# Attention scores of a graph layer: from sums of rows and columns to products of exponentials, spread through DRAM

## The chip, the cores and the metric

The kernel runs on one core of a Trainium2 chip. The metric is the time of one execution on the device in microseconds (us). Its engines are TensorE (PE; its weight loads are shown apart as PEld), VectorE (DVE), ScalarE (ACT), GpSimd (POOL) and SyncE (SP, which here only issues DMAs). Each runs its own instructions in order; semaphores tie them together.

## The reference

For 64 graphs of 256 nodes with 256 features: a graph-attention layer pair (GAT) with a feed-forward part, then a relational attention layer with a feed-forward part. The change touches only the GAT softmax, which runs twice per graph:

```python
def _gat(h, adj, W, a, out_features):
    Wh = jnp.matmul(h, W)
    Wh1 = jnp.matmul(Wh, a[:out_features])
    Wh2 = jnp.matmul(Wh, a[out_features:])
    e = Wh1 + jnp.swapaxes(Wh2, 1, 2)
    e = jax.nn.leaky_relu(e, negative_slope=ALPHA)      # ALPHA = 0.2
    scores = jnp.where(adj > 0, e, NEG)
    att = jax.nn.softmax(scores, axis=1)
    return jnp.matmul(att, Wh)
h = _gat(x, adj, W1, a1, Fout)
h = _gat(h, adj, W2, a2, W2.shape[1])
h = _layernorm(residual + h, g_ln1, b_ln1)
```

After it come a ReLU feed-forward (256 to 1024 to 256) with a layernorm, then 8-head attention whose weights are masked by the relation, a projection, a layernorm, a GELU feed-forward and a layernorm. All values are float32.

## The kernel before

**Tiles.** Two graphs make a group (G = 2, 512 nodes), so there are 32 groups. The nodes of a group lie on 128 partitions in T = 4 blocks, two blocks a graph (NB = 2). "Transposed" tiles such as `xT` and `hT` hold features on partitions.

**The pipeline.** `turn(y_, x_, z)` (L1226) is one turn of the main loop (L1533) and works on three groups at once: group `y_` is in its relational attention and GELU feed-forward, group `x_ = y_ + 1` in the ReLU feed-forward, group `z = y_ + 2` in its two GAT layers. So 30 of the 32 groups pass their GAT layers in a turn; groups 0 and 1 do it ahead of the loop (L1499 to L1510). In the turns where all three groups exist, the order of PE, SP, DVE and ACT is the order in which `turn` writes the instructions (L1271). Where a step is placed in `turn` is therefore where it stands in the queue of each engine.

**Group z in a turn.** `early` transposes the loaded x, `project` (L1145) multiplies it by the weights and two score vectors into `xp` (a 128x260 product and an ACT copy per block; the last columns hold the row and column scores). It is split: two blocks ahead of `first("4b")`, two blocks behind `out_(0)`. `first_scores` (L1149) makes a `Softmax` object for layer 1, and `score_rows` (L745) turns the row scores on PE: four transposes of a column that is repeated 128 times give a PSUM bank with the row of 512 scores on every partition. Then per graph `b`:

- `scores(b)` (L764): ACT adds the column score as a bias to the row for two blocks (L766), DVE applies the leaky function over 128x512 (L768).
- `exp(b)` (L770): ACT takes the exponential over 128x512.
- `masks(b)` (L773): DVE multiplies each block by the adjacency and sums the block's rows into `z` (L775).

`shares` (L778) inverts `z`, `scaled` (L789) multiplies xp by it on ACT, and `first_sums` (L1167) multiplies the scores with xp on PE (`hpp`, L800) into `hp`. Layer 2 does the same from `hp`: `second_scores` is called after the GELU part, its `scores` and `exp` stand between the products of the second feed-forward, and `second_sums` (`ygp`, L811) ends it.

**Neighbours in the queues.** Between those steps stand the other groups' steps. `sums(n)` are the attention sums of a head group on PE (`po`, `zo`), `shares(b)` their division on DVE (L1123 to L1128), `out_(b)` the output projection with its addition (L814). `first(...)` and `second(...)` are the seven products of a Strassen-like hidden layer (`hidden_seven`, L869): products 1, 6, 7, 4 accumulate in one PSUM bank and DVE adds that bank into `h` after 1, 6 and 7 (L910), before the next product goes into it; 2, 5, 3 use another bank, copied by ACT (L907). `out(n)` and `out.sums(n)` are the seven products of the output layer (L987), their additions (L995) and operand sums (L973). `normed_features` (L689) transposes 32x32 squares on DVE (L694) and places them with 12 DMAs and four POOL copies (L713, L711); layer `2` splits the DMAs between SP and ACT. `stored` and `load_rows` issue the 512 KB store of a finished group (L1202) and the 512 KB load of the next rows (L441) on SP. `affine` is two DVE passes over 128x1024 (L864, L867).

**Buffers.** SBUF tiles come from pools by tag; tag `es` has two buffers of 4 KB a partition and serves the sums over nodes and the division; tag `v` has one, shared by the values of the attention and the scores `s`. PSUM tag `g` has six banks, which all of the above share.

Of the kernel before, what the change touches and what calls it, by code (L numbers as in the profile page):

```python
# [9 lines left out]
F32 = mybir.dt.float32  # L10
I32 = mybir.dt.int32
AF = mybir.ActivationFunctionType
ALU = mybir.AluOpType
# [3 lines left out]
P = 128  # L17
NEG = -9000000000000000.0
ALPHA = 0.2
# [366 lines left out]
def narrow_path(  # L386
# [13 lines left out]
    nc = tc.nc  # L400
    B, N, F = x.shape
# [3 lines left out]
    KB = F // P  # L405
    FB = FF // P
    NB = N // P
    G = 2
    T = G * NB
    TN = G * N  # L410
# [68 lines left out]
    high = const.tile([P, T], F32, name="high")  # L479
    nc.gpsimd.memset(high, 0.0)  # L480
    other = const.tile([P, NG], F32, name="other")

    def weight(w, name):
        t = const.tile([P, w.shape[0] // P, w.shape[1]], F32, name=name)
# [172 lines left out]


    mark = {}

    def behind(*names):

# [82 lines left out]
    def score_rows(u, l, wh, c):  # L745

        rows = bank(f"rows{u}_{l}")
        for t in range(T):
            nc.tensor.transpose(rows[:, t * P:(t + 1) * P],
                                wh[:, t, c:c + 1].to_broadcast([P, P]), ident)  # L750
        return rows

    class Softmax:

        def __init__(s, u, l, wh, rows, c):
            s.u, s.wh, s.rows, s.c = u, wh, rows, c
# [4 lines left out]
        def block(s, b):  # L761
            return s.s[:, b * NB:(b + 1) * NB, :].rearrange("p t n -> p (t n)")

        def scores(s, b):  # L764
            for t in range(b * NB, (b + 1) * NB):
                nc.scalar.activation(s.s[:, t, :], s.rows[:, b * N:(b + 1) * N], AF.Identity,  # L766
                                     bias=s.wh[:, t, s.c:s.c + 1])
            nc.vector.scalar_tensor_tensor(s.block(b), s.block(b), ALPHA, s.block(b), op0=ALU.mult, op1=ALU.max)  # L768

        def exp(s, b):  # L770
            nc.scalar.activation(s.block(b), s.block(b), AF.Exp)

        def masks(s, b):  # L773
            for t in range(b * NB, (b + 1) * NB):
                nc.vector.scalar_tensor_tensor(s.s[:, t, :], s.s[:, t, :], 1.0, g[s.u]["aT"][:, t, :],  # L775
                                               op0=ALU.mult, op1=ALU.mult, accum_out=s.z[:, t:t + 1])
# [4 lines left out]

        def all(s):
            for b in range(G):
                s.scores(b)
                s.exp(b)
                s.masks(b)
            s.shares()

# [69 lines left out]
    def affine(y, g_, b_):  # L858

        times(y, g_)  # L860
        plus(y, b_)
# [144 lines left out]
    class Projections:  # L1006
# [111 lines left out]
    def divided(u, b, po, zo, oT):  # L1118


        rz = work.tile([P, KB * N], F32, tag="es", name=f"rz{u}_{b}")
        rq = work.tile([P, KB * N // 32], F32, tag="rq", name=f"rq{u}_{b}")
# [22 lines left out]
    def project(z, blocks=range(T)):  # L1145
        d = g[z]
        d["xp"] = projected(z, d["xT"], blocks, d.get("xp"))

    def first_scores(z):  # L1149
        d = g[z]  # L1150
        d["m"] = Softmax(z, 0, d["xp"], score_rows(z, 0, d["xp"], F + 2), F + 3)

    def second_scores(z):
        d = g[z]
        d["m"] = Softmax(z, 1, d["hp"], score_rows(z, 1, d["hp"], F), F + 1)

    def first_softmax(z):
        first_scores(z)
# [67 lines left out]
    def turn(y_, x_, z):  # L1226
# [46 lines left out]
        with order:  # L1273
# [73 lines left out]
            masks(3)  # L1347
            totals(3)
            if Z:
                project(z, range(0, T // 2))  # L1350
            first("4b")
            sums(2)
            sums(3)
# [5 lines left out]
                    out.sums(1, 2)  # L1359
            if Z:  # L1360
                shares(1)
            out_(0)
            if Z:
                mv = moments(y_, 2, y, range(NB))
# [1 line left out]
                n = norm(y_, 2, y, range(NB))  # L1366
            piece()
            if Z:
                project(z, range(T // 2, T))
            if Z:  # L1370
                early_adjacency(z)
            elif X:
                out.sums(1)
                out(1, 2)
                out.sums(2)
            out_(1)
            piece()
            if Z:
                first_scores(z)
            if Z:  # L1380
                n = norm(y_, 2, y, mv=mv)
            else:
                applied_norm(y, *n)
                n = norm(y_, 2, y, range(NB, T))
            if Z:
                out(1)
                Z["m"].scores(0)
                Z["m"].scores(1)
                Z["m"].exp(0)
                Z["m"].exp(1)  # L1390
                out.sums(4)
                out(2, 5)
            elif X:
                out(5)
                out.sums(3)
# [31 lines left out]
                n = moments(x_, 1, X["y"], range(NB))  # L1427
            if Z:
                first_sums(z, range(T // 2, T))
            if X:  # L1430
                out.product(4)
            tt = work.tile([P, HPB, NB * N], F32, tag="e", name=f"tt{y_}_1")
            second = hidden_seven(y_, 1, hT, w1s, b1, AF.Gelu, Y, tt.rearrange("p a n -> p (a n)"))
            if X:
                out.add(4)
                n = norm(x_, 1, X["y"], mv=n)
# [5 lines left out]
                applied_norm(X["y"], *n, [0])  # L1442
            if Z:
                affine(y, rg3, rb3)
            second("3a")
            if X:
                applied_norm(X["y"], *n, [1])
# [11 lines left out]
            if y_ >= NG - 2:  # L1459
# [129 lines left out]
```

## Time and profile before

| | |
|---|---|
| median of 3 runs | 3045.75 us (3045.45 to 3047.17) |
| profiled execution | 3043.91 us |
| its span | 3042.3 us |
| granted TensorE clock | 0.995 |
| ACT busy / POOL busy | 1684.9 us / 679.8 us |
| row transposes (L749), modelled busy | 39.9 us in 256 instructions |
| leaky function on DVE (L768) | 92.4 us in 128 |
| exponentials (L771) | 76.5 us in 128, and 30 table loads of 1283 ns |
| masks (L775) | 98.9 us with 128 accumulator reads |
| score biases on ACT (L766) | 100.3 us in 256 |

The profile is one execution recorded by the hardware. Its page gives each engine's busy time, the chain of work that ended last, the groups of instructions by line with their mean duration, and the DMA issues with their time to landing. A timeline shows one engine's instructions in order: start, length, engine, line, operation, tile written <- tiles read, shape, count, and in brackets how long the engine stood idle before it and what ended the idle time. PE's ends are modelled and overlap, so on PE the distance between two starts is the measure.

### The profile page before, as it was taken

Reading aid. Unit: us, or ns where it says so; the run is one execution under the profiler, and the core shown is the slowest. Engines: PE = TensorE matmul, PEld = TensorE weight load, DVE = VectorE, ACT = ScalarE, POOL = GpSimd, SP = SyncE. Lnnn points to the kernel's source line nnn. Section 1 sums busy time; section 2 is a strip of 40 time slices with the busy share of each in tenths; the row PEclk is TensorE's granted clock in tenths of the full one; section 3 lists DMA queues with packets and bytes.
Section 4 is the critical chain, followed back from the end, with each engine's and each line's share of the span. In section 5 each row is a group of like instructions: output and inputs, shape, how many; then the busy total and the mean of one; then the engine's idle time right before and its main releaser. Section 6 shows DMA issues by size and latency. Waiting matters only on the chain.

```text
span 3042.3 us, 58414 instructions
## 1 busy us (share of the span) xinstructions
PE 3000.0 (99%) x22192; PEld 2459.6 (81%) x22192; DVE 2645.7 (87%) x5025; ACT 1684.9 (55%) x3404; POOL 679.8 (22%) x930
## 2 busy tenths in 40 slices
PE   7999999999999999999999999999999999999998
PEld 6788888888787888787888878887878887878876
DVE  5788988888898889898889888898988898988887
ACT  4455555655655555555555455556555555555553
POOL 4222221222211222212222112222112222122211
PEclk8999999999999999999999999999999999999999
DMA  5011111211111211111111112111112111121000
GB/s 147 13 35 36 37 39 25 44 37 39 34 35 32 44 37 39 33 27 43 40 37 36 40 25 44 38 39 33 34 35 44 36 38 35 25 45 37 19 13 16
DMA packets 428402, 113.24 MB, mean 37 GB/s; under 512 B 364586, under 2 KB 427604, under 8 KB 428116
## 3 DMA queue, kind: packets, MB, share of 16 engines
q1 hardware_dynamic: 418076, 102.20, 15.3%
q10 hardware_dynamic: 8984, 6.19, 0.8%
q8 instruction: 178, 2.92, 0.4%
q0 software_dynamic: 1056, 1.05, 0.1%
q14 instruction: 108, 0.88, 0.1%
HBM read 56.78 MB, written 16.78 MB: 24 GB/s over the span
## 4 chain that ended last, share of the span: by engine, by line
PE 90%; DVE 7%; ACT 1%; DMA 1%; POOL 1%; issue 0%; SPq 0%; DVEq 0%; POOLq 0%; ACTq 0%
PE yf L987 22%; PE h1a L898 15%; PE h1b L898 12%; PE po L1112 8%; PE qk L1053 7%; PE v L1053 7%; PE sp L1084 4%; PE xpp L740 4%; PE yop L811 4%; PE ygp L811 3%; PE zo L1115 2%; PE hpp L800 2%; DVE s L775 2%; DVE yt L694 1%; DVE eaq L973 1%; DVE y L995 1%
## 5 line engine op out<-in xcount | busy, mean ns | idle before, releaser
L907 ACT COPY h<-h1b 128x512 f32<-128x512 f32 x384 | 224.5, 585 | 349.4 <-PE h1b L898 342.6
L910 DVE TENSOR_TENSOR h<-h1a,h 128x512 f32<-128x512 f32 x384 | 262.9, 685 | 114.6 <-PE h1a L898 108.8
L1097 DVE TENSOR_TENSOR ea<-e,aT 128x1024 f32<-128x1024 f32 x256 | 311.2, 1237 | 2.9 <-ACT e L1093 2.6
L855 ACT ACTIVATE y<-y,nm,rs 128x256 f32<-128x256 f32 x450 | 249.8, 597 | 114.4 <-DVE nm L845 110.1
L1093 ACT ACTIVATE e<-sp 128x512 f32<-128x512 f32 x512 | 270.8, 600 | 28.1 <-PE sp L1084 21.4
L1036 ACT COPY qk<-qk 128x512 f32<-128x512 f32 x128 | 75.1, 587 | 339.0 <-PE qk L1053 339.0
L711 POOL COPY hT<-yt 32x256 f32<-32x256 f32 x244 | 203.2, 833 | 184.9 <-DVE yt L694 172.6
L837 POOL TENSOR_SCALAR rs<-mv 128x4 f32<-128x4 f32 (+1 forms) x134 | 33.3, 248 | 841.0 <-DVE mv L827 625.3
L826 DVE BATCH_NORM_STATS2 st<-y 128x6 f32<-128x256 f32 x512 | 207.3, 407 | 4.5
L995 DVE TENSOR_TENSOR y<-yf,y 128x256 f32<-128x256 f32 x448 | 183.2, 409 | 29.5 <-PE yf L987 29.4
L1125 POOL TENSOR_TENSOR low<-low,rq 128x16 f32<-128x16 f32 x64 | 13.9, 218 | 810.4 <-DVE rq L1124 810.4
L867 DVE TENSOR_TENSOR y<-y,rb 128x1024 f32<-128x1024 f32 (+1 forms) x130 | 167.0, 1284 | 3.2
L941 ACT ACTIVATE h<-h,cols 128x512 f32<-128x512 f32 x256 | 167.0, 714 | 1.5 <-DVE h L910 1.1
L864 DVE TENSOR_TENSOR y<-y,rg 128x1024 f32<-128x1024 f32 (+1 forms) x130 | 161.6, 1243 | 1.2 <-ACT y L855 1.1
L1102 DVE TENSOR_TENSOR es<-e 128x1024 f32<-128x1024 f32 x128 | 155.8, 1217 | 0.0
L703 POOL COPY hT<-yt 32x256 f32<-32x256 f32 x120 | 114.9, 958 | 169.3 <-DVE yt L694 165.1
L838 POOL TENSOR_TENSOR rs<-rs,mhalf 128x4 f32<-128x4 f32 (+1 forms) x134 | 146.9, 1096 | 8.3
L1084 PE MATMUL sp<-qk 32*128 32x256 f32 x2048 | 146.6, 400 | 0.4 <-DVE qk L1040 0.3
L742 ACT COPY xp<-xpp 128x260 f32<-128x260 f32 x128 | 45.4, 385 | 172.6 <-PE xpp L740 172.5
L694 DVE STREAM_TRANSPOSE yt<-y 128x256 f32<-128x256 f32 x364 | 136.0, 418 | 4.5
L1112 PE MATMUL po<-e,v 128*32 128x256 f32 x2048 | 136.3, 384 | 0.0
L898 PE MATMUL h1a<-tt,wf 128*128 128x256 f32 x512 | 134.2, 386 | 0.3 <-DVE h L910 0.3
(280 smaller groups left out, 7589.6 us busy)
## 6 DMA issues: line engine op xcount, KB each, us to landing
hT<-yt SPq DMA_DIRECT2D x912, 32.0 KB, 1.9
y<-in_x_dram SPq DMA_DIRECT2D x32, 512.0 KB, 4.5
xq<-in_x_dram SPq DMA_DIRECT2D x240, 64.0 KB, 2.1
aq<-in_adj_dram SPq DMA_DIRECT2D x240, 64.0 KB, 2.3
out_dram<-y SPq DMA_DIRECT2D x30, 512.0 KB, 2.9
hT<-yt ACTq DMA_DIRECT2D x180, 32.0 KB, 1.9
wf<-in_L_gnn_w_ff_dram SPq DMA_DIRECT2D x2, 1024.0 KB, 7.6
w<-in_L_gnn_W_dram SPq DMA_DIRECT2D x2, 1024.0 KB, 7.9
```

The source lines that it names most:

```text
L811: nc.tensor.matmul(ps[:, i * F:(i + 1) * F], lhs(t, k), rhs(b, k), start=(k == 0), stop=(k == n - 1))
L855: mark["normed"] = nc.scalar.activation(y[:, t, :], y[:, t, :], AF.Identity, bias=nm[:, t:t + 1], scale=rs[:, t:t + 1])
L898: nc.tensor.matmul(ps[:, i * N:(i + 1) * N], w_[:, f * P:(f + 1) * P], m, start=first and i == 0, stop=True, skip_group_check=True)
L907: mark["copied"] = nc.scalar.copy(out(h, o, b), pair(ps))
L910: mark["added"] = nc.vector.tensor_tensor(out(h, o, b), pair(one[h]), out(h, o, b), ALU.add)
L987: nc.tensor.matmul(s.ps[n][:, i * F2:(i + 1) * F2], a[:, k, i * P:(i + 1) * P], w_[:, k, :], start=n in (1, 2, 5) and i == 0 and k == 0, s ...
L995: mark["out"] = nc.vector.tensor_tensor(yq, s.ps[n][:, :F].rearrange("p (i f) -> p i f", i=NB), yq, ALU.add)
L1053: nc.tensor.matmul(ps[:, i * N:(i + 1) * N], l, r, start=n in (1, 2, 5) and i == 0, stop=True, skip_group_check=True)
L1084: nc.tensor.matmul(ps[a][:, j * N:(j + 1) * N], k_[hp, m, j0:j0 + P], q[hp, m, b * N:(b + 1) * N], start=True, stop=True)
L1093: nc.scalar.activation(e[:, a, :], ps[a], AF.Exp, scale=isd)
L1097: nc.vector.tensor_tensor(ea[:, a:a + 2, :], e[:, a:a + 2, :], ab[:, None, :].to_broadcast([P, 2, NB * N]), ALU.mult)
L1112: nc.tensor.matmul(po[hp, m * N:(m + 1) * N], vs[:, hp], w[:, a, j * N:(j + 1) * N], start=(n == 0), stop=(n == len(terms) - 1))
```

## The change

The identity used is exp(leaky(r + c)) = max(exp(r) exp(c), exp(0.2 r) exp(0.2 c)), and a factor exp(c) that is common to a softmax row cancels: the weight becomes max(exp(r), exp(0.2 r) f) with f = exp(-0.8 c). So only the row and column scores are exponentiated, 128x4 numbers each, not the 256x256 sums.

- In groups 2 to 31, ACT takes three exponentials of 128x4 columns: `f`, and `k` with exp(r) and exp(0.2 r). `rows` (a new method) transposes `k` on DVE in 32x32 squares (each column repeated 32 times), writes the 1024 numbers to a line in DRAM by one DMA from four partitions, and reads that line onto all 128 partitions by a second DMA (512 KB, 4 KB a partition). Both are issued by SP.
- In groups 0 and 1 the rows are still turned by PE, and ACT exponentiates the PSUM bank twice.
- `masks(b)` makes each block by one DVE instruction (multiply by `f`, then the larger of that and the other row) before it multiplies by the adjacency as it did.
- The leaky function, the 128x512 exponentials and the Identity activations of `scores` are gone.
- `project(z)` is in one piece ahead of `first("4b")`, followed by `first_scores`; `rows` of layer 1 stands behind `shares(1)`; `out(1)` takes the place of the second half of the projection.
- `second_scores` stands right behind `first_sums`, its `rows` behind the operand sums of the second hidden layer, `masks(0)` of layer 2 between that layer's fifth and third products.
- A tiny exponential `warm` on ACT stands where the scores of layer 2 were exponentiated.
- The tile `rq` has one buffer in place of two.

```diff
+    dram = ctx.enter_context(tc.tile_pool(name="lines", bufs=2, space=bass.MemoryType.DRAM))
...
+        def __init__(s, u, l, wh, r):
...
+            nc.scalar.activation(s.f, wh[:, :, r + 1], AF.Exp, scale=ALPHA - 1.0)
+            if u > 1:
+                s.k = work.tile([P, 2, T], F32, tag="ek", name=f"ek{u}_{l}", bufs=1)
+                for n, scale in enumerate((1.0, ALPHA)):
+                    nc.scalar.activation(s.k[:, n], wh[:, :, r], AF.Exp, scale=scale)
+            else:
+                rows = score_rows(u, l, wh, r)
+                er = work.tile([P, 2, TN], F32, tag="es", name=f"er{u}_{l}")
+                for n, scale in enumerate((1.0, ALPHA)):
+                    nc.scalar.activation(er[:, n], rows, AF.Exp, scale=scale)
+                s.e = [er[:, n] for n in range(2)]
+
+        def rows(s):
+
+            tr = work.tile([P, 2 * T, 32], F32, tag="es", name=f"tr{s.n}")
+            nc.vector.transpose(tr, s.k.rearrange("p e t -> p (e t)")[:, :, None].to_broadcast([P, 2 * T, 32]))
+            er = work.tile([P, 2, T, Q, 32], F32, tag="es", name=f"er{s.n}")
+            line = dram.tile([2 * T, Q, 32], F32, tag="line", name=f"ln{s.n}")
+            nc.sync.dma_start(line.rearrange("n a y -> a n y"), tr[::32])
+            nc.sync.dma_start(er.rearrange("p e t a y -> p (e t a y)"),
+                              bass.AP(tensor=line.tensor, offset=line.offset, ap=[[0, P], [1, 2 * TN]]))
+            s.e = [er[:, n].rearrange("p t a y -> p (t a y)") for n in range(2)]
+
+        def masks(s, b):
+            bn = slice(b * N, (b + 1) * N)
             for t in range(b * NB, (b + 1) * NB):
-                nc.scalar.activation(s.s[:, t, :], s.rows[:, b * N:(b + 1) * N], AF.Identity,
-                                     bias=s.wh[:, t, s.c:s.c + 1])
-            nc.vector.scalar_tensor_tensor(s.block(b), s.block(b), ALPHA, s.block(b), op0=ALU.mult, op1=ALU.max)
-
-        def exp(s, b):
-            nc.scalar.activation(s.block(b), s.block(b), AF.Exp)
-
-        def masks(s, b):
+                nc.vector.scalar_tensor_tensor(
+                    s.s[:, t, :], s.e[1][:, bn], s.f[:, t:t + 1], s.e[0][:, bn], op0=ALU.mult, op1=ALU.max)
...
             if Z:
-                project(z, range(0, T // 2))
+                project(z)
+                first_scores(z)
             first("4b")
...
             if Z:
                 shares(1)
+                Z["m"].rows()
             out_(0)
...
             if Z:
-                project(z, range(T // 2, T))
-            if Z:
+                out(1)
                 early_adjacency(z)
...
-            if Z:
-                first_scores(z)
...
             if Z:
-                out(1)
-                Z["m"].scores(0)
-                Z["m"].scores(1)
-                Z["m"].exp(0)
-                Z["m"].exp(1)
                 out.sums(4)
                 out(2, 5)
...
                 first_sums(z, range(T // 2, T))
+                second_scores(z)
...
             second = hidden_seven(y_, 1, hT, w1s, b1, AF.Gelu, Y, tt.rearrange("p a n -> p (a n)"))
+            if Z:
+                Z["m"].rows()
...
                 affine(y, rg3, rb3)
+                Z["m"].masks(0)
             second("3a")
...
-            second_scores(z)
...
-            Z["m"].scores(0)
             out.add(1)
             out.product(5)
-            Z["m"].scores(1)
-            Z["m"].exp(0)
-            Z["m"].exp(1)
+            nc.scalar.activation(warm, mhalf[:, 0:1], AF.Exp)
             checked(z, Z["aq"])
...
-            Z["m"].masks(0)
             out(6)
             Z["m"].masks(1)
```

More of the change, by code (lines that the diff above doesn't have):

```diff
@@ L481, in narrow_path @@
     other = const.tile([P, NG], F32, name="other")
+    warm = const.tile([P, 1], F32, name="warm")
     def weight(w, name):
@@ L753, in narrow_path @@
     class Softmax:
-        def __init__(s, u, l, wh, rows, c):
-            s.u, s.wh, s.rows, s.c = u, wh, rows, c
+        def __init__(s, u, l, wh, r):
+            s.u, s.wh, s.n = u, wh, f"{u}_{l}"
             s.s = (work.tile([P, T, N], F32, tag="v", name=f"s{u}_{l}", bufs=1) if u > 1 else
@@ L759, in __init__ @@
             s.z = work.tile([P, T], F32, tag="z", name=f"z{u}_{l}")
-        def block(s, b):
-            return s.s[:, b * NB:(b + 1) * NB, :].rearrange("p t n -> p (t n)")
-        def scores(s, b):
-            for t in range(b * NB, (b + 1) * NB):
-                nc.scalar.activation(s.s[:, t, :], s.rows[:, b * N:(b + 1) * N], AF.Identity,
-                                     bias=s.wh[:, t, s.c:s.c + 1])
-            nc.vector.scalar_tensor_tensor(s.block(b), s.block(b), ALPHA, s.block(b), op0=ALU.mult, op1=ALU.max)
@@ L770, in exp @@
-        def exp(s, b):
-            nc.scalar.activation(s.block(b), s.block(b), AF.Exp)
-        def masks(s, b):
+            s.f = work.tile([P, T], F32, tag="ef", name=f"ef{u}_{l}", bufs=1)
+            nc.scalar.activation(s.f, wh[:, :, r + 1], AF.Exp, scale=ALPHA - 1.0)
[9 more added lines that the diff above has]
+                s.e = [er[:, n] for n in range(2)]
@@ L783, in all @@
             for b in range(G):
-                s.scores(b)
-                s.exp(b)
                 s.masks(b)
@@ L1121, in divided @@
         rz = work.tile([P, KB * N], F32, tag="es", name=f"rz{u}_{b}")
-        rq = work.tile([P, KB * N // 32], F32, tag="rq", name=f"rq{u}_{b}")
+        rq = work.tile([P, KB * N // 32], F32, tag="rq", name=f"rq{u}_{b}", bufs=1)
         nc.vector.transpose(rz, zo)
@@ L1150, in first_scores @@
         d = g[z]
-        d["m"] = Softmax(z, 0, d["xp"], score_rows(z, 0, d["xp"], F + 2), F + 3)
+        d["m"] = Softmax(z, 0, d["xp"], F + 2)
     def second_scores(z):
         d = g[z]
-        d["m"] = Softmax(z, 1, d["hp"], score_rows(z, 1, d["hp"], F), F + 1)
+        d["m"] = Softmax(z, 1, d["hp"], F)
     def first_softmax(z):
```

## The prediction

> **What bounds the kernel now.** I read the page first (busy shares, chain), then one settled turn of the loop as a timeline engine by engine, then the DMA issues.
>
> The page:
>
> ```profile
> span 3042.3 us, 58414 instructions
> ...
> PE 3000.0 (99%) x22192; PEld 2459.6 (81%) x22192; DVE 2645.7 (87%) x5025; ACT 1684.9 (55%) x3404; POOL 679.8 (22%) x930
> ...
> PE 90%; DVE 7%; ACT 1%; DMA 1%; POOL 1%; issue 0%; SPq 0%; DVEq 0%; POOLq 0%; ACTq 0%
> ```
>
> TensorE (PE) is never really idle, so a matmul removed is time saved, and anything that makes PE wait is time added. DVE at 87% is second. ACT at 55% has room.
>
> PE in the turn from 1033.34 to 1125.91 us (pitch 92.57 us; the turns around 812, 1459 and 2105 us show the same pattern):
>
> ```profile
> 1080.09 0.60 PE L749 MATMUL rows<-ident,xp 128*128 128x128 f32 x4
> 1080.52 3.74 PE L987 MATMUL yf<-wf,h 128*128 128x128 f32 x32
> 1084.10 3.74 PE L987 MATMUL yf<-wf2t,eq 128*128 128x128 f32 x32
> 1087.67 1.95 PE L987 MATMUL yf<-wf,eaq 128*128 128x128 f32 x16
> 1089.46 1.91 PE L800 MATMUL hpp<-xp,s 128*128 128x258 f32 x8
> ...
> 1103.86 1.89 PE L898 MATMUL h1a<-tt,w1s 128*128 128x256 f32 x8
> 1105.74 3.91 PE L898 MATMUL h1a<-tt,w 128*128 128x256 f32 x16
> 1109.48 0.60 PE L749 MATMUL rows<-ident,hp 128*128 128x128 f32 x4
> 1109.92 1.95 PE L987 MATMUL yf<-w,h 128*128 128x128 f32 x16
> ```
>
> Differences of starts are the real cost, since the ends overlap: the four row transposes cost 0.43 us and 0.44 us of PE, twice a turn. Two places have no slack. The aggregation `hpp` starts at 1089.46, when ACT has only just scaled xp (ACT L791 runs from 1088.59). Products 6a/6b need 1.88 us instead of 1.73 before 7a starts at 1105.74, because 7a waits for DVE's addition of 6a.
>
> DVE in the same turn:
>
> ```profile
> 1084.06 1.22 DVE L973 TENSOR_TENSOR eaq<-h,eq 128x1024 f32<-128x1024 f32 x1
> 1085.19 0.41 DVE L995 TENSOR_TENSOR y<-yf,y 128x256 f32<-128x256 f32 x1
> 1086.08 0.42 DVE L995 TENSOR_TENSOR y<-yf,y 128x256 f32<-128x256 f32 x1 [0.48 <-PE yf L987]
> 1086.42 0.15 DVE L845 SCALAR_TENSOR_TENSOR nm<-mv,rs 128x4 f32<-128x4 f32 x1
> ...
> 1102.53 1.47 DVE L867 TENSOR_TENSOR y<-y,rb 128x1024 f32<-128x1024 f32 x1
> 1104.99 0.69 DVE L910 TENSOR_TENSOR h<-h1a,h 128x512 f32<-128x512 f32 x1 [1.00 <-PE h1a L898]
> ```
>
> DVE has only 0.48 us of idle time ahead of the first layer's masks and 1.00 us ahead of the addition of 6a. These two gaps are all the cover that the new DVE work has.
>
> DMA issues (KB, us to landing), and SP around the second layer:
>
> ```profile
> hT<-yt SPq DMA_DIRECT2D x912, 32.0 KB, 1.9
> y<-in_x_dram SPq DMA_DIRECT2D x32, 512.0 KB, 4.5
> ...
> out_dram<-y SPq DMA_DIRECT2D x30, 512.0 KB, 2.9
> ```
>
> ```profile
> 1094.70 0.54 SPq L1202 DMA_DIRECT2D out_dram<-y  x1
> 1097.71 0.39 SPq L441 DMA_DIRECT2D y<-in_x_dram  x1
> ```
>
> The 512 KB load of the next rows goes out at 1097.71 (4.4 us to landing), just where the second layer's new DMAs will stand.
>
> **What the Trainium skill says.** "DMA: Bandwidth & Descriptors", section "Anatomy of one DMA", puts about 2.0 us fixed cost on a DMA, mostly the receipt of the write; the trace agrees (1.9 us for 32 KB). The same page, "Queues, rings and completion order": "On each SDMA engine descriptors are consumed in ring order", so a small DMA issued by SP behind a large one waits for it. The trace points the same way: at the start a 128 KB row load behind two 1 MB weights took 8.0 us, another 4.1. "ScalarE: Activation LUTs", "What ACT_TABLE_LOAD costs", has 1283 ns a load, the trace 1283 exactly, and 186 ns + 0.833 ns an element for an ACTIVATE without pointer operands: an estimate of 0.19 us for each new 128x4 exp, which the trace before does not show.
>
> **The change, part by part**, with the turn above as the clock.
>
> (1) Row transposes leave PE in 30 of 32 groups: 30 x (0.43 + 0.44) = 26 us saved if nothing else waits. The freed PSUM bank is worth nothing: I see no bank wait over 0.3 us here.
>
> (2) ACT loses four Identity (1.57 us) and two exps (1.2 us) a layer, gains three tiny exps (0.6 us by the estimate; 0 to 1). With 55% busy this is worth nothing directly. Table loads stay two a turn: `warm` takes the exp load (1.28 us) where L771 had it. They don't add.
>
> (3) DVE a layer: away two 128x512 leaky ops (1.28 us in layer 1), in come a 128x256 transpose (0.33 us pitch, as L694) and four 128x256 maxima. Their nearest row is L775, same engine, form and size: 0.345 us pitch, so 1.38 us. Net +0.43 us. More important is the place: the leaky ops ran early; the maxima sit directly in front of the masks.
>
> (4) First layer. The second half of the projection (1.75 us of PE) moves ahead of sums(2) and sums(3), so zo ends near 1076.5 instead of 1074.7 and DVE starts shares(1) at 1076.5, not 1075.34. From there its queue is solid, from its own rows: shares 2.38, transpose 0.35, out_(0) add and moments 1.78, add(1) 0.34, adjacency 1.14, out_(1) add and moments 1.85, sums(4) 1.13, two adds 0.68, which is 1086.15. The norm offset waits for GpSimd's pow (moments end + 2.0 us, as before) to 1086.4. Masks take 8 x 0.345 = 2.76, the reciprocal 0.15: 1089.4. ACT scales two blocks by 1090.4, and hpp's four first products end at 1091.75, 0.3 us later than before although PE was ready 0.43 earlier. DVE's transposes for hT end at 1091.15 instead of 1089.8, so all 12 hT DMAs, and SP behind them, slide by 1.35 us; the second hidden stage starts at 1097.45 instead of 1096.87. The broadcast itself is hidden: transpose out by 1079.3, line landed 1081.3 (1.9 us), spread landed 1085.7 (4.4 us), needed at 1086.5.
>
> (5) Second layer. SP's order is: hT, store, load of the rows, line, spread. The load now goes out at 1097.71 + 1.35 = 1099.05; DVE's transpose is done at 1099.25; so the line is issued right behind 512 KB. With ring order it lands when that load does, 1103.45. SP waits for it and then issues the spread. Its 512 KB in 4 KB pieces is not in the trace: lower bound the 512 KB store, 2.9 us; upper bound by the nearest row, 4.4 us with its 1 KB pieces; I take 4.0. Landed at 1107.5. DVE reaches masks(0) at 1105.1 (the affine 2.7 us behind the offset at 1102.4), so it waits 2.4 us; masks(0) 1.38, addition of 6a 0.69: 7a can start at 1109.6. PE was ready at 1106.3. Queued behind the waiting DVE: the additions of 6a, 6b, 7a, 7b, and behind those GELU and the output sums. Some turns (812, 2105) issue the load 0.7 us earlier; mean about 1109.25. Against 1105.74 that is +3.5; 0.43 comes back with the removed transposes: **+3.1 us a turn**. The rest of the turn has no new wait: the leaky ops and masks(0) have left DVE there, and the GELU chain shifts no more than PE does.
>
> (6) Prologue: groups 0 and 1 keep the PE transposes; ACT 2.8 us becomes two PSUM exps (1.2 us), DVE slightly more. I take -2 us (0 to -6).
>
> Sum: 28 turns x 3.1 = +87; the first and last such turns have no store or load in front of the line, and DVE alone costs about +1.2 each; prologue -2. Against the profiled execution (3043.91 us, of which the span is 3042.3): 3043.9 + 87 + 2.4 - 2 = 3131. The median of the runs is 1.8 us above that execution: **3133 us**.
>
> **The rivals.**
>
> A, the forecast (0.53): the line queues behind the row load. With the spread at 2.9 to 4.4 us and +-0.4 us on the queue sums, 2.0 to 3.9 us a turn: 3100 to 3155.
>
> B (0.25): the line is not held up by the load. It lands 1.9 us after issue (1101.4), the spread at 1105.4 to 1105.8, just when DVE arrives. Then only DVE's extra work counts: 7a at about 1107.2 to 1107.9, +1.0 to +1.7 a turn, 3074 to 3100; with a little more slack than I found, 3065. For it: the line needs few pieces and SP issues it just 0.4 us behind the load. Against: the ring order above.
>
> C, the other side, faster (0.10): PE is still the only bound, because DVE has more slack than my sums give it. Place: the addition of 6a. It decides from the point where the spread has landed and the affine is over by 1104.2, so that 7a starts at 1106.3, and where the first layer's masks are over by 1088. Then the 26 us are saved: 3045.75 - 26 - 2 = 3018. For it: 99% busy PE, 13% idle DVE. Against: both gaps on DVE are smaller than the work put in them.
>
> D (0.12): 128 reads of one 4 KB line are slower than an ordinary load. At 6.4 us (2 more) the first layer's masks are 1.2 us late too and the second layer's 3.6: about 6 us a turn, 3045.75 + 30 x 6 - 2 = 3224. Against: the 128 KB row broadcasts at the start ran within a stretch of 350 to 371 GB/s.
>
> Some 0.2% (6 us) is what a measurement of this kernel can tell from no change; between B and C I leave 0.03 for that, out of their 0.35. Chances: faster 0.09, same 0.03, slower 0.88.
>
> The range leaves out C and most of D: 3070 to 3180, which holds A, nearly all of B and the near end of D.
>
> **What would show it.** PE idle in front of hpp (about 0.7 us, on ACT xp) and in front of 7a (about 3 us, on DVE's addition into h); DVE idle in front of the second layer's first maximum, on the DMA er, about 2 us, and none in the first layer; line landing about 4 us in layer 2 and 2 us in layer 1; PE busy some 26 us less; maxima at about 0.41 us each. I am wrong if the line lands in 2 us in both layers (B), if PE shows no wait at 7a (C), or if DVE waits for er in the first layer as well (D).

## The result and the profile after

The changed kernel takes 3158.44 us (median of 4 runs, 3156.53 to 3164.04) against 3045.61 us (3045.45 to 3047.17) for the kernel before on the same chip: ratio 1.0373, interval 1.0356 to 1.0389. It is 112.8 us slower; the forecast was 3133 us with 3070 to 3180 as its range.

The head of the page of the kernel after: span, busy times, and the chain of work that ended last.

```profile
span 3154.9 us, 58139 instructions
...
PE 2987.0 (95%) x21952; PEld 2444.4 (77%) x21952; DVE 2688.9 (85%) x5213; ACT 1545.3 (49%) x3242; POOL 681.8 (22%) x930
...
PE 66%; DVE 19%; DMA 8%; POOL 2%; issue 2%; SPq 1%; ACT 1%; ACTq 0%; DVEq 0%; POOLq 0%
```

PE falls from 99% to 95% busy, and its part of the chain from 90% to 66%; DVE and DMA have taken over. PE has less work, and waits for more than it lost. What it waits for stands in the list of PE's waits of the kernel after (us in total, times, longest):

```profile
PE hpp L819 <- ACT xp L810: 51.0, 30, 1.8
PE h1a L917 <- DVE h L929: 50.4, 31, 3.5
PE yf L1006 <- DVE eaq L992: 20.4, 30, 0.7
```

Three waits a turn, 121.8 us in all. In the same list of the kernel before only the second has an entry, of 1.0 us in 3 times; that list begins with a 6.1 us wait of the prologue and goes on with sums of 4.9 us and less. The three are, in order of a turn: ahead of the aggregation (1.70 us, layer 1), ahead of output product 7 (0.68 us, layer 1) and ahead of hidden product 7a (1.63 us in the turn below, layer 2).

The turn that follows is the counterpart of the one in the prediction. I measure both from the start of the PE instruction `sp` just ahead of the turn's first projection (1066.43 us before, 1103.04 us after):

| PE instruction | before | after | slip |
|---|---|---|---|
| aggregation `hpp`, first half | 23.03 | 24.45 | 1.42 |
| output product 7 (`yf<-wf,eaq`, the second such) | 25.02 | 27.13 | 2.11 |
| second hidden stage, first product (`h1b<-hT,w`) | 30.44 | 32.55 | 2.11 |
| hidden product 7a | 39.31 | 43.06 | 3.75 |
| next turn's first `qk` | 59.48 | 62.84 | 3.36 |

So layer 1 costs 2.11 us and layer 2 another 1.64, of which 0.39 comes back. From the loop's first projection to its last, 29 pitches sum to 2681.9 us before and 2790.0 us after (+108.1, or 3.73 a turn); the first such projection starts 2.2 us later, and what lies behind the last is 2.3 us longer.

**Layer 1.** PE of the kernel after in that turn:

```profile
1123.84 1.95 PE L1006 MATMUL yf<-wf,eaq 128*128 128x128 f32 x16
1127.49 2.01 PE L819 MATMUL hpp<-xp,s 128*128 128x258 f32 x8 [1.70 <-ACT xp L810]
1130.17 2.05 PE L1006 MATMUL yf<-wf,eaq 128*128 128x128 f32 x16 [0.68 <-DVE eaq L992]
```

DVE in the same stretch tells why (`...` stands for rows left out):

```profile
1113.27 0.72 DVE L1142 STREAM_TRANSPOSE rz<-zo 128x512 f32<-128x512 f32 x1 [0.90 <-PE zo L1134]
...
1115.74 0.43 DVE L782 STREAM_TRANSPOSE tr<-ek 128x256 f32<-128x256 f32 x1
...
1121.11 1.19 DVE L992 TENSOR_TENSOR eaq<-h,eq 128x1024 f32<-128x1024 f32 x1
1122.22 0.75 DVE L1014 TENSOR_TENSOR y<-yf,y 128x256 f32<-128x256 f32 x2
1123.55 0.16 DVE L864 SCALAR_TENSOR_TENSOR nm<-mv,rs 128x4 f32<-128x4 f32 x1 [0.57 <-POOL rs L857]
1123.63 0.88 DVE L793 SCALAR_TENSOR_TENSOR s<-er,ef 128x256 f32<-128x256 f32 x2
...
1126.71 0.18 DVE L800 RECIPROCAL z<-z 128x4 f32<-128x4 f32 x1
...
1128.76 1.36 DVE L992 TENSOR_TENSOR eaq<-h 128x1024 f32<-128x1024 f32 x1
```

and of the kernel before:

```profile
1087.99 0.18 DVE L779 RECIPROCAL z<-z 128x4 f32<-128x4 f32 x1
...
1090.04 1.36 DVE L973 TENSOR_TENSOR eaq<-h 128x1024 f32<-128x1024 f32 x1
```

Three things are to be seen: DVE idles 0.90 us for `zo`, which the whole projection has pushed back; it idles 0.57 us for GpSimd's pow (the power of -0.5 in the layernorm); and the four maxima (0.395 us each: the next row begins 0.79 us behind a pair) stand between the offset and the masks' sums. The reciprocal that ends the masks starts at 23.67 us of the turn against 21.56 before: 2.11 us late, exactly PE's slip. The first maximum does not wait for `er`: the spread has landed in time. Product 7 waits because its operand `eaq` is the next DVE work behind the masks and the transposes of `yt`. Before, DVE kept the same distance (3.4 us from the reciprocal's start to the end of that `eaq`), but there ACT was still normalizing when the reciprocal came, and the aggregation itself started 0.7 us later against it. So both waits of layer 1 are one slip of DVE.

**Layer 2.** SP of the kernel after, first the line and the spread of layer 1, then what it issues around those of layer 2:

```profile
1116.20 0.59 SPq L785 DMA_DIRECT2D ln<-tr  x1
1117.98 0.35 SPq L786 DMA_DIRECT2D er<-ln  x1
...
1132.93 0.52 SPq L1221 DMA_DIRECT2D out_dram<-y  x1
1135.99 0.40 SPq L441 DMA_DIRECT2D y<-in_x_dram  x1
1136.86 0.59 SPq L785 DMA_DIRECT2D ln<-tr  x1
1140.11 0.34 SPq L786 DMA_DIRECT2D er<-ln  x1
```

and DVE and PE where the line is used:

```profile
1143.87 0.88 DVE L793 SCALAR_TENSOR_TENSOR s<-er,ef 128x256 f32<-128x256 f32 x2 [1.16 <-DMA er<-ln]
...
1145.36 1.28 DVE L929 TENSOR_TENSOR h<-h1a,h 128x512 f32<-128x512 f32 x2
```

```profile
1142.58 1.89 PE L917 MATMUL h1a<-tt,w1s 128*128 128x256 f32 x8
1146.10 3.91 PE L917 MATMUL h1a<-tt,w 128*128 128x256 f32 x16 [1.63 <-DVE h L929]
```

The line goes out 0.87 us behind the 512 KB row load, and SP can issue the spread only when the line has landed: 3.25 us later. In layer 1, with nothing ahead of it, the same pair stands 1.78 us apart. The spread then takes 3.76 us until DVE goes on at 1143.87. DVE has waited 1.16 us, spends 1.49 us on masks(0), and only then comes the addition of 6a that releases 7a.

### The profile page after: what moved, and what is told of

Same layout as the page of the kernel before. It is cut to its first block, busy times and chain, and to the rows that moved or that the text cites. A ratio compares the mean times of both kernels' runs of the same rounds, so it can differ in the third digit from the quotient of the medians.

```text
span 3154.9 us, 58139 instructions
## 1 busy us (share of the span) xinstructions
PE 2987.0 (95%) x21952; PEld 2444.4 (77%) x21952; DVE 2688.9 (85%) x5213; ACT 1545.3 (49%) x3242; POOL 681.8 (22%) x930
## 4 chain that ended last, share of the span: by engine, by line
PE 66%; DVE 19%; DMA 8%; POOL 2%; issue 2%; SPq 1%; ACT 1%; ACTq 0%; DVEq 0%; POOLq 0%
PE yf L1006 14%; PE h1a L917 12%; PE po L1131 7%; PE h1b L917 7%; PE qk L1072 7%; PE v L1072 6%; PE sp L1103 4%; PE xpp L742 4%; PE ygp L830 3%; DMA er<-ln 3%; DMA ln<-tr 3%; DVE s L793 3%; DVE s L796 2%; DVE st L845 2%; PE zo L1134 2%
## 5 line engine op out<-in xcount | busy, mean ns | idle before, releaser
L856 POOL TENSOR_SCALAR rs<-mv 128x4 f32<-128x4 f32 (+1 forms) x134 | 57.8, 431 | 877.4 <-DVE mv L846 641.8
L713 POOL COPY hT<-yt 32x256 f32<-32x256 f32 x244 | 203.3, 833 | 184.1 <-DVE yt L696 132.1
L917 PE MATMUL h1a<-tt,w 128*128 128x256 f32 x512 | 132.7, 411 | 50.4 <-DVE h L929 50.4
L819 PE MATMUL hpp<-xp,s 128*128 128x258 f32 x512 | 126.2, 391 | 51.0 <-ACT xp L810 51.0
L917 PEld LDWEIGHTS h1a<-tt,w 128*128 128x128 f32 x512 | 96.0, 201 | 86.8 <-DVE h L929 71.8
L705 POOL COPY hT<-yt 32x256 f32<-32x256 f32 x120 | 104.6, 872 | 222.5 <-DVE yt L696 209.8
L793 DVE SCALAR_TENSOR_TENSOR s<-er,ef 128x256 f32<-128x256 f32 x256 | 116.4, 495 | 38.7 <-DMA er<-ln 33.6
L1006 PE MATMUL yf<-wf,eaq 128*128 128x128 f32 x1024 | 127.6, 278 | 21.5 <-DVE eaq L992 20.4
```

Of the source, the lines that this page charges most:

```text
L793: nc.vector.scalar_tensor_tensor(s.s[:, t, :], s.e[1][:, bn], s.f[:, t:t + 1], s.e[0][:, bn], op0=ALU.mult, op1=ALU.max)
L917: nc.tensor.matmul(ps[:, i * N:(i + 1) * N], w_[:, f * P:(f + 1) * P], m, start=first and i == 0, stop=True, skip_group_check=True)
L1006: nc.tensor.matmul(s.ps[n][:, i * F2:(i + 1) * F2], a[:, k, i * P:(i + 1) * P], w_[:, k, :], start=n in (1, 2, 5) and i == 0 and k == 0, s ...
```

## The experiments

Ratios are against the kernel before, on the same chip. In the diffs, lines with a minus are those of the changed kernel.

**Which layer costs what.** Two kernels have one layer in the old form and the other in the new. In the first, layer 1 is the old one; the loop's `scores`, `exp`, the projection in two halves and the row transposes stand where they were, and layer 2 is new:

```diff
-        d["m"] = Softmax(z, 0, d["xp"], F + 2)
+        if z > 1:
+            d["m"] = OldSoftmax(z, 0, d["xp"], score_rows(z, 0, d["xp"], F + 2), F + 3)
+        else:
+            d["m"] = Softmax(z, 0, d["xp"], F + 2)
...
```

> Layer 1 of groups 2 to 31 as before (row transposes on PE, split projection, Identity, leaky, exp), layer 2 as changed. My theory (two stalls that add up: a late DVE queue ahead of hpp in layer 1, and a line held up by the row load plus the maxima ahead of the addition of 6a in layer 2): only the wait ahead of 7a stays, about 2 us a turn less 0.44 us for the transposes, so 3082 to 3096 us, and no PE wait at hpp. Rival (layer 2 only inherits the slip of layer 1): PE no longer waits at 7a and 13 us are saved, about 3033 us.

Measured: 3091.67 us (3090.04 to 3096.72), ratio 1.0158 (1.0141 to 1.0175): +47.4. PE's list of waits has the one of layer 2 alone:

```profile
PE h1a L949 <- DVE h L961: 49.6, 32, 2.8
```

In the second, layer 1 is the new one and layer 2 the old one:

```diff
-        d["m"] = Softmax(z, 1, d["hp"], F)
+        if z > 1:
+            d["m"] = OldSoftmax(z, 1, d["hp"], score_rows(z, 1, d["hp"], F), F + 1)
+        else:
+            d["m"] = Softmax(z, 1, d["hp"], F)
...
```

> Layer 1 as changed, layer 2 of groups 2 to 31 as before. My theory: in the turn at 1103 us of the changed kernel the start of the second hidden layer had slipped by 2.1 us against before; that remains and nothing is added at 7a, so 30 x 2.1 = 63 us: about 3108 us. If the two layers' stalls don't add but hide each other, more: 3130 us or above. If layer 1 costs what the prediction said (0.6 us a turn), about 3064 us.

Measured: 3109.13 us (3108.27 to 3110.29), ratio 1.0214 (1.0197 to 1.0231): +64.8. Its list has the other two, unchanged:

```profile
PE hpp L851 <- ACT xp L810: 50.8, 30, 1.7
PE yf L1038 <- DVE eaq L1024: 20.4, 30, 0.7
```

47.4 and 64.8 make 112.2, against 112.8 measured for both: the two layers' costs add up, and neither hides behind the other. Layer 1, for which I had set 0.6 us a turn, is the dearer one.

**The order in SP's queue.** The load of the next rows is issued behind the line and the spread of layer 2 instead of ahead of them:

```diff
-            if z + 1 < NG:
-                load_rows(z + 1)
             if Z:
                 first_sums(z, range(0, T // 2))
...
                 Z["m"].rows()
+            if z + 1 < NG:
+                load_rows(z + 1)
```

> The changed kernel, with the 512 KB load of the rows issued by SP behind the second layer's line and spread instead of ahead of them. My theory (the line waits in the ring for that load): SP's step from the line to the spread falls from 3.2 to about 1.8 us in layer 2, DVE's wait for er (33.6 us) goes, PE's wait ahead of 7a falls by 1.2 us a turn: about 3123 us. Rival (the line is slow there for another reason, such as the write to DRAM itself): the step stays at 3.2 us and the time within 6 us of 3158.

Measured: 3120.8 us (3120.69 to 3122.28), ratio 1.0253 (1.0236 to 1.027): 37.6 less than the changed kernel. SP of this kernel in the same turn:

```profile
1128.03 0.59 SPq L785 DMA_DIRECT2D ln<-tr  x1
1129.74 0.33 SPq L786 DMA_DIRECT2D er<-ln  x1
1130.16 0.39 SPq L441 DMA_DIRECT2D y<-in_x_dram  x1
```

The same line with the same bytes now takes 1.71 us instead of 3.25, so it was the load ahead of it, and not the write to DRAM, that held it up. Whether the line waits its turn behind the load in the queue, or only shares the DMA engines with it, this run does not separate. DVE hardly waits for `er` any more (2.1 us in all against 33.6), but a wait at 7a is left:

```profile
PE h1a L917 <- DVE h L929: 20.9, 31, 1.3
```

That is 0.7 us a turn: masks(0), put ahead of the addition of 6a, takes DVE's time there even when its data has come.

**That place.** masks(0) of layer 2 goes back to where the kernel before has it, behind the hidden stage:

```diff
                 affine(y, rg3, rb3)
-                Z["m"].masks(0)
...
             out(2)
+            Z["m"].masks(0)
             out(6)
```

> The changed kernel, with masks(0) of layer 2 where it was before the change, ahead of out(6) in the second output layer. My theory: nothing of layer 2 stands ahead of the addition of 6a any more, PE's wait at 7a (1.63 us in the turn looked at) goes and nothing waits at ygp: 3158 - 49 = about 3109 us. Rival (DVE simply has too much to do, wherever it stands): the wait comes back ahead of ygp and the time stays above 3145 us.

Measured: 3119.93 us (3119.16 to 3120.63), ratio 1.0249 (1.0232 to 1.0266). The wait at 7a is gone altogether, with the line still behind the load, since there is time for it now. But the time is 11 us above the 3109 I expected, and above the kernel with the old layer 2. The removed row transposes of layer 2 gain nothing even here. PE's list shows where they went:

```profile
PE yf L1006 <- DVE eq L992: 6.9, 30, 0.4
```

Output product 5 starts at 47.34 us of the turn (from 1094.03 us), in the kernel with the old layer 2, transposes and all, at 47.38 (from 1089.86). It needs DVE's sum `eq`, and that waits for ACT's GELU. DVE of this kernel, and of the kernel before:

```profile
1140.00 1.23 DVE L992 TENSOR_TENSOR eq<-h 128x1024 f32<-128x1024 f32 x1 [0.49 <-ACT h L935]
```

```profile
1110.29 1.23 DVE L973 TENSOR_TENSOR eq<-h 128x1024 f32<-128x1024 f32 x1 [0.50 <-ACT h L916]
```

The wait for ACT was there before the change as well; the row transposes only filled PE's time until the sum was there. Behind it, `ygp` starts another 0.2 us later against product 5, behind the two maxima of masks(1) and the scaling.

**The place of the projection.** Its second half goes back behind the attention sums. That is later than in the changed kernel, but not yet its old place: the kernel before has it behind `out_(0)`.

```diff
-                project(z)
-                first_scores(z)
+                project(z, range(0, T // 2))
             first("4b")
             sums(2)
             sums(3)
+            if Z:
+                project(z, range(T // 2, T))
+                first_scores(z)
```

> The second half of the projection goes back behind sums(2) and sums(3), as in the kernel before; the rest is the changed kernel. My theory (the moved projection holds up DVE's first share transpose by 0.90 us, and from there to the scaling of xp DVE has no slack): 0.9 us a turn less, PE idle ahead of the aggregation 1.70 -> about 0.8 us, and since everything behind shifts alike, the waits ahead of output product 7 (0.68) and ahead of 7a (1.6) stay: 3158 - 27 = 3131 us, 3120 to 3140. Rival (the aggregation is held up by GpSimd's pow and the row-wise norm, not by the moved projection): the wait of DVE on the pow grows by what DVE gains, 3150 or more.

Measured: 3131.78 us (3129.31 to 3134.62), ratio 1.0286 (1.0269 to 1.0303): 26.7 less. The idle time ahead of `zo` is gone, and the waits at product 7 and 7a stay, as expected. PE's wait ahead of the aggregation is 1.08 instead of 1.70 us; not 0.8, because the projection now stands ahead of `yop`, for which DVE waits 0.33 us. So the time came out as expected in part by luck: the aggregation starts 0.62 us a turn earlier, some 19 us in all and not 27. Shorter waits at 7a (47.1 us in sum against 50.4) and fewer of the falls of the clock described at the end (three against five) make up most of the rest.

**The idle time on the pow.** `tops(b)`, a method of its own for the first loop of `masks(b)`, makes the two maxima of a half; that of the first half stands ahead of the norm offset, where DVE waited for GpSimd:

```diff
+            if Z:
+                Z["m"].tops(0)
             applied_norm(y, *n)
```

> The two maxima of the first layer's first half stand ahead of the norm offset instead of behind it; all else as in the changed kernel. Theory (DVE idles 0.57 us on the pow, just in front of its critical work): the two maxima (0.8 us) fill the gap, the masks end about 0.57 us earlier, the offset goes out only 0.2 us later and ACT's normalization stays ahead of the scaling: 0.5 to 0.6 us a turn, 3140 to 3145 us. Rival (ACT, which normalizes four blocks before it scales xp, is what the aggregation waits for next): no gain, 3155 to 3165 us.

Measured: 3132.99 us (3128.93 to 3133.67), ratio 1.0292 (1.0274 to 1.0309): 25.4 less, more than the 13 to 18 I expected. In the turn shown the aggregation starts 0.68 us earlier and 7a 1.11, since layer 2's line and DVE come earlier too. The clock falls three times here as well, not five.

**Layer 1 with both cures, layer 2 old.** The last two edits are called the cures below. Both, as in their diffs, in the kernel with the old layer 2:

```diff
+                project(z, range(T // 2, T))
+                first_scores(z)
...
+                Z["m"].tops(0)
```

> First layer in the new form with both cures (projection in two halves, the first two maxima ahead of the norm offset), second layer in the old form: four identities, leaky op, exps, row transposes on PE. Against the same without the cures (3109.1 us) the gain should be the sum, 0.9 + 0.55 us a turn: 3066 us, 3055 to 3080; PE idle ahead of the aggregation at most 0.4 us, ahead of output product 7 still 0.5 to 0.7. That is still above the kernel before, since the maxima themselves (0.4 us of DVE more) stay on the path. Rival: with the cures the first layer costs DVE nothing that PE sees, and the removed row transposes show as a gain: 3030 to 3040 us.

Measured: 3081.29 us (3080.83 to 3083.1), ratio 1.0123 (1.0106 to 1.014): 27.8 less than without the cures, where I expected 43. They do not add up: singly they brought the aggregation forward by 0.62 and 0.68 us, together by 0.96, and PE's wait ahead of it stays at 0.73 us.

And with the second half of the aggregation ahead of product 7:

```diff
                 first_sums(z, range(0, T // 2))
+                first_sums(z, range(T // 2, T))
                 out(7)
...
-            if Z:
-                first_sums(z, range(T // 2, T))
...
```

> As the one before it, and besides output product 7 stands behind the whole aggregation instead of between its halves, so that PE has work while DVE makes the sum that product 7 reads. If the 0.68 us wait there is an order that PE could avoid: 0.5 to 0.7 us a turn less, 3045 to 3055 us. Rival: the wait goes, but the addition of product 7 reaches DVE 0.9 us later and with it the affine, and the addition of 6a in the second hidden stage (1.00 us of idle time ahead of it in the kernel before) is late instead: no gain, within 8 us of the one before it.

Measured: 3075.09 us (3074.55 to 3075.49), ratio 1.01 (1.0083 to 1.0117): 6 us less, as the rival's number, but not by its mechanism. The wait at product 7 is gone, and most of it appears one product later, where `yf` waits 0.52 us for DVE's addition into `y`; 7a does not wait.

**The old place of the projection.** What keeps the aggregation 0.45 us late was still open. This kernel, again with the old layer 2, gives the projection and output product 1 the places they had before the change. The new operations of layer 1 follow the projection, and the first two maxima stay ahead of the norm offset:

```diff
-                project(z)
-                first_scores(z)
+                project(z, range(0, T // 2))
...
-                Z["m"].rows()
             out_(0)
...
-                out(1)
+                project(z, range(T // 2, T))
+                first_scores(z)
+                Z["m"].rows()
                 early_adjacency(z)
...
+                out(1)
                 out.sums(4)
                 out(2, 5)
```

> First layer in the new form, second layer in the old one, as e10; but the second half of the projection stands where the kernel before has it, behind the first attention output product, with the new scores and the turn through DRAM behind it, and output product 1 back behind the norm; the first two maxima stay ahead of the norm offset. In e10 DVE waited another 0.33 us for the first attention output product (yop) and the norm started accordingly later. Theory: the places that the edit moved, and not the new operations, cost the first layer nearly all it lost; the aggregation starts within 0.3 us of where the kernel before has it, since ACT (normalize 2.08, scale 1.7 us) is then its last releaser as it was there: 3044 us, 3035 to 3058; the 0.44 us a turn of row transposes turns into a PE wait of about that size ahead of the aggregation. Rival: the maxima, 0.4 us more of DVE work than the leaky ops, and the later line keep the aggregation 0.7 us or more late: 3065 us or more.

Measured: 3080.5 us (3079.95 to 3081.84), ratio 1.0121 (1.0106 to 1.0137): the same as the one with the projection elsewhere. My expectation (3035 to 3058) is wrong; the rival's time fits, and of its two reasons the maxima, since DVE does not wait for `er` here. The aggregation starts at 23.48 us of the turn in both kernels (from 1080.76 us here, from 1081.38 in the kernel with both cures), though DVE is less occupied in this one. DVE of this kernel:

```profile
1099.98 0.43 DVE L1052 TENSOR_TENSOR y<-yf,y 128x256 f32<-128x256 f32 x1 [0.95 <-PE yf L1044]
1100.32 0.87 DVE L794 SCALAR_TENSOR_TENSOR s<-er,ef 128x256 f32<-128x256 f32 x2
1101.10 0.16 DVE L902 SCALAR_TENSOR_TENSOR nm<-mv,rs 128x4 f32<-128x4 f32 x1
1101.18 0.42 DVE L802 SCALAR_TENSOR_TENSOR s<-s,aT 128x256 f32<-128x256 f32 x1
```

In front of the maxima DVE adds output product 5, and that comes when PE has made it: the addition starts at 19.22 us of the turn here and at 19.21 in the kernel with both cures. From there run two maxima, two masks, two maxima, two masks and the scaling to 23.48. Before, the addition stood at 19.65 and only four masks followed. So the transposes that PE no longer makes do bring the addition 0.43 us earlier, and the maxima behind it, 4 x 0.395 = 1.58 us, take that, the 0.7 us for which ACT, still normalizing, once let the finished masks wait, and the 0.45 us by which the aggregation is late. This is a sum of places in the traces; no run takes the maxima away alone. They can't simply go into the 0.95 us ahead of the addition: line and spread go out at 1094.37 and 1096.13, and 3.76 us behind that, as long as the spread of layer 2 took, is 1099.9. Whether they could with an earlier line wasn't tried.

**The same layer 1 with the new layer 2**, its masks(0) late as above:

```diff
-                Z["m"].masks(0)
...
             out(2)
+            Z["m"].masks(0)
```

> The same first layer, and the second layer in the new form with its first masks put back behind the additions of the hidden stage (as in e2). Theory: e2 against e6 had the new second layer 0.36 us a turn above the old one when no wait stands at 7a, so about 11 us above e12: 3055 us, 3043 to 3070. Rival: where the first layer no longer holds up DVE, the second layer's removed row transposes show as a gain too: 3035 us or less.

Measured: 3090.49 us (3090.02 to 3091.61), ratio 1.0154 (1.014 to 1.0168): 10 us above the kernel with the old layer 2, as expected. The time itself lies outside the 3043 to 3070, which had been built on the wrong expectation for the kernel before this one. No version with either layer in the new form came back to the time before; the nearest stayed 30 us above it. Two things were not run: the maxima with the row transposes left on PE, and the line issued from another engine's queue while the load is under way.

## Why the prediction was right, and where its steps were not

The sign, the mechanism of layer 2 and the range were right; the point was 25 us low. That it came so close is luck: layer 1 was set too low by 1.5 us a turn and layer 2 too high by 1.25, and the two errors nearly cancel.

- (1) **Row transposes, 26 us saved if nothing else waits.** The condition failed twice over, and with it the sentence that a matmul removed is time saved. In layer 1 the 0.43 us show only as an earlier addition of product 5; in layer 2 they were PE's filling while ACT's GELU and DVE's sum were under way. Modelled PE busy time fell by 13.0 us, not 26; rows that begin after a wait are longer (2.01 against 1.91 us for `hpp`), so the page does not separate the saving.
- (2) **ACT's relief, worth nothing:** held. ACT falls from 1684.9 to 1545.3 us busy, and the time rises. Each 128x4 exponential took 0.19 to 0.21 us, as estimated.
- (3) **DVE, net +0.43 us a layer.** Mis-sized: a maximum takes 0.395 us of DVE and not the 0.345 of the masks that I took as its nearest row, so 1.58 us and net +0.66 in layer 1 (with the transpose at 0.36).
- (4) **Layer 1, "the second hidden stage starts +0.6 us".** This is the step that failed: 2.11. Two parts make it up. The reciprocal was to start 1.2 us late, and comes 2.11 late. Of the difference, 0.2 is the maxima of (3), and another 0.2 are the offset itself and the step to the reciprocal, which my sum left out. The norm offset, which I had at the place it had before, comes 0.52 us later: the moments in front of it end 0.2 us later than in my sum, and the offset follows them by 2.4 us instead of the 2.0 I copied (why, the last section shows). Second, I had counted the transposes of `yt` and the hT DMAs as late without following the `eaq` sum behind them to product 7; that wait is the 0.68. With it even my own reciprocal would have put the second hidden stage 1.2 us late and not 0.6. The wait ahead of the aggregation is 1.70, not 0.7. Right in it: the idle time for `zo` that the projection makes, and the hidden spread.
- (5) **Layer 2, the line behind the load.** Right in that the load holds up the line, as turning the order round showed. The line had landed 4.1 us after the load's issue (4.4 in my sum); in the 28 turns with a load ahead line and spread stand 3.3 to 3.8 us apart, in the two without one 1.7. The spread took 3.76 us (4.0). Too large was the wait: 1.16 us on `er` and 1.63 at 7a, not 2.4 and 3. I had let layer 1 delay the load by 1.35 us and PE by only 0.6; in the turn shown the load is 1.67 us late and PE 2.11, so PE comes later to a 7a that starts where my sum had it (43.06 us of the turn, 43.2 in the sum). The wait does not depend on layer 1's slip: with the old layer 1 it was 49.6 us in all, with the new one 50.4. Net of what comes back, layer 2 costs 1.25 us a turn, not 2.5.
- The turn's sum of **+3.1 us** was thus close (3.36 in the turn shown, 3.73 on the mean) with wrong shares. Of the remaining 25 us the halved clock below makes some 8, the turn's own 0.26 us some 7, the prologue 4 and what lies behind the loop 2.
- (6) **Prologue, -2 us:** wrong in sign. The loop's first projection starts 2.2 us later.
- Of the rivals, B (the line not held up) and D (a slow spread, DVE waiting for `er` in layer 1 too) fall by the same lines; C, no wait at 7a, falls by the 50.4 us of waits there.

## What to carry to other kernels

An engine that shows 99% busy does not make its work worth its full price: ask for each removed instruction what the next one waits for, since a removed matmul may have been filling the time until another engine was done. Where work moves to an engine with a queue as full as DVE's here, follow everything behind it in that queue to its reader, not just the first: here product 7 waited for a sum that stood behind the transposes I had followed. A small DMA issued right behind a large one in the same queue took about the large one's time here (3.25 us against 1.71), so a value that another engine waits for is better issued ahead of the loads that have time.

## What the runs showed that I had not expected

GpSimd makes the norm's factor by a small addition and the pow behind it. The addition took 0.24 us before and 1.04 us after. GpSimd of the kernel before, of the kernel after, and of the kernel with the old place of the projection:

```profile
1082.68 0.24 POOL L837 TENSOR_SCALAR rs<-mv 128x4 f32<-128x4 f32 x1 [5.98 <-DVE mv L827]
1083.00 1.43 POOL L838 TENSOR_TENSOR rs<-rs,mhalf 128x4 f32<-128x4 f32 x1
```

```profile
1121.36 1.04 POOL L856 TENSOR_SCALAR rs<-mv 128x4 f32<-128x4 f32 x1 [6.71 <-DVE mv L846]
1122.48 1.03 POOL L857 TENSOR_TENSOR rs<-rs,mhalf 128x4 f32<-128x4 f32 x1
```

```profile
1097.41 0.23 POOL L894 TENSOR_SCALAR rs<-mv 128x4 f32<-128x4 f32 x1 [6.38 <-DVE mv L884]
1097.73 1.85 POOL L895 TENSOR_TENSOR rs<-rs,mhalf 128x4 f32<-128x4 f32 x1
```

In the kernel after, the addition begins while DVE makes `eaq` from two SBUF tiles (1121.11 to 1122.30) and ends right behind it, at 1122.40. All 30 turns show this, with 1.04 us each; in the same kernel the addition takes 0.23 to 0.25 us where DVE is adding out of PSUM. In the third kernel `eaq` runs from 1097.47 to 1098.69 and begins behind the start of the addition: that keeps its 0.23 us, and the pow, which begins beside the sum, takes 1.85 us. So the delay goes where that sum goes. The Trainium skill, "SBUF — State Buffer", section "Who interferes with whom", says that DVE and GpSimd share one port pair and that "only the shared port pair causes contention, and it's an exclusive lock". These rows agree with it. Addition and pow together take 1.75 us before and 2.15 after: these are the 0.4 us by which the norm offset of (4) came later behind the moments than I had copied.

Second, the granted clock. In the kernel after TensorE's clock falls to half for 3.4 us in five turns of the loop, each about 1 us or less behind the end of one of the longer waits at 7a (1.97 to 3.54 us). Windows of 1 us behind the wait that ended at 1048.86 (length; busy time of PE, PEld, DVE, ACT and POOL, each with its number of instructions; the granted clock; the DMA engines' share and GB/s):

```profile
1049.00:1050.00 1.00, 1.00 (x5) 0.90 (x6) 0.40 (x1) 1.00 (x2) 0.00 (x0) 0.97 0.00 0
1050.00:1051.00 1.00, 1.00 (x4) 0.72 (x4) 0.69 (x1) 1.00 (x3) 0.00 (x0) 0.50 0.00 0
1051.00:1052.00 1.00, 1.00 (x4) 0.81 (x3) 0.35 (x1) 1.00 (x3) 0.00 (x0) 0.50 0.00 0
```

That turn takes 97.58 us, its neighbour 95.82. The kernel before has none in its loop, nor have the kernels whose wait at 7a is gone or cut to 0.7 us; the three others have three or five. Half of 3.4 us, five times, is an estimate of some 8 us of the loss. It fits the run with the load behind, where the waits at 7a fell by 29.5 us in sum, all five falls of the clock went, and the time fell by 37.6 us. Four other waits of 1.95 us and more were not followed by one, so what sets it off stays open.
